# The first six A^T steps of the first pass are transposed and cast in the last block of the set-up, and written from SyncE's queue

## The chip, the cores and the metric

The kernel runs on one core of one Trainium2 chip. The time is the device time of one execution in microseconds (us). Engines are called as in the profile: PE is TensorE (PEld its weight loads), DVE is VectorE, ACT is ScalarE, POOL is GpSimd, SP is SyncE. SP only starts transfers here; POOL does small arithmetic and starts transfers too. All times inside an execution are counted from the start of the profiled span.

## The reference, cut to what matters

Two layers work on 4096 nodes with 512 features each. Layer 0 is a graph attention with 8 heads of 64 features over a 4096 x 4096 adjacency matrix of zeros and ones; layer 1 is an attention inside 32 groups of 128 nodes. The change touches layer 0 only:

```
feats   = einsum('nf,hfo->hno', X, W)                 # per head
s_self  = einsum('hno,ho->hn', feats, a_self)
s_neigh = einsum('hno,ho->hn', feats, a_neigh)
dense   = s_self[:, :, None] + s_neigh[:, None, :]
dense   = where(dense > 0, dense, 0.2 * dense) * A
attn    = softmax(dense, axis=-1)
out     = relu(concat_heads(attn @ feats) + b)
x       = layernorm(x + out)
```

Layer 1 then computes `layernorm(x + softmax(...) @ value)` with scores that are masked to the own group.

## The kernel before

**Layer 0 is streamed over the transposed adjacency matrix.** The exponentials of the two scores are taken once per node, so that a product of two exponentials stands for each entry, and a comparison ("mark") says on which side of the leaky ReLU an entry is. The kernel makes four passes, `main_pass(0)` to `main_pass(3)`, each for one pair of heads. A pass has four chunks `c` of 1024 target nodes, and a chunk has 32 steps `j` of 128 source nodes. One step needs `ats[r, c, j]`, a 128 x 1024 float32 tile of A^T.

**How a tile of A^T comes about.** In the first pass `bring(0, c, j)` makes two steps at once: eight PE transposes (L1122) of an fp8 block `a_b`, with two fp8 values taken as one bf16 value, into one PSUM bank that `misc` hands out; then two ACT copies (L1126, "CAST at<-ps_m") that widen them to float32 in SBUF; then, for each, a write to the scratch tensor `at_d` in HBM (L1127, started by POOL). In later passes `bring` only reads `at_d` back through SP. The block `a_b` is loaded by POOL in `load_adjacency` (L596); the first three are requested in blocks 3, 4 and 5 of the set-up.

**What a step does with it.** DVE computes `q` (L1361), two of them per step; ACT (L1370) or, for one in eight, DVE (L1366) computes the marks; PE then runs matmuls into `accf` (L1381, 4 per step, needs only the A^T tile), `acc` (L1401, 16 per step, needs `q`), `dens` (L1415, needs the marks) and, in the first pass, `ae` (L1325). In the first three passes the steps are taken in groups of eight (`wide=8`): all `accf` matmuls of a group, half of the next group's `bring`, all `acc` matmuls, the `dens` and `ae` matmuls, the other half of `bring`. Only the first group of all has no group ahead of it that could bring its tiles. It does so itself, before its first matmul:

```
                if at_step == 0:
                    for j in cycle:
                        bring(0, 0, j)
```

**The set-up ahead of the first pass** has eight blocks `k` of four row tiles. In each block PE computes features of tile `u` (`features(k, u)`, 4 matmuls, L743), DVE adds the bias (`fb`, L751), DVE and ACT make two scaled copies (`gst`, L757; `fst`, L765 and L766), and POOL writes them to HBM (`g_d`, `f_d`, L778). `exponentials`, `scores`, `turn_rows`, `rows_of_exponentials` and `columns_of_exponentials` stand between them. After the last block (k = 7) PE has `sums_to_columns` (L583) and `columns_of_exponentials(7)` (L735); DVE reads these from PSUM (`S_col` L819, `pu_all` L736), clears `dens` (L826), and the PSUM banks of the set-up go over to the passes.

**What sets the order.** PE runs its instructions exactly in program order (`manual_schedule`). For ACT, DVE, POOL and SP a planner fixes the order when the program is built, from program order and from when it reckons an operand to be ready, and it moves later work ahead where it sees a gap: the loads `p_row<-pu_d` and `f_s<-f_d` of the first pass are started from 42 us on, in the middle of the set-up.

**Buffers.** The `at` tiles have six buffers (`atp`) that exist from the beginning, and six more (`at2`) that are allocated when the set-up's SBUF pools are closed; `ring` takes them in turn, so steps 0 to 5 use the first six, steps 6 and 7 the later ones. `q` has six early and two later buffers. During the set-up `misc` has one PSUM bank, from the first pass on two. `fst`, `gst` and `fb` have three buffers each in the set-up, so the fourth tile waits until the first has been written to HBM.

Of the kernel before, what the change touches and what calls it, by code (L numbers as in the profile page):

```python
# [10 lines left out]
F32 = mybir.dt.float32  # L11
BF16 = mybir.dt.bfloat16
# [7 lines left out]
P = 128  # L20
# [375 lines left out]
F32R = mybir.dt.float32r  # L396
# [8 lines left out]
def adjacency_streamed_path(  # L405
# [29 lines left out]
    nc = tc.nc  # L435
# [8 lines left out]
    FP8 = mybir.dt.float8e4  # L444
    C = 1024
    CT = C // P
# [18 lines left out]
    at_d = dram.tile([NCH, NT, P, C], F32, name="at_d")  # L465
# [30 lines left out]
    ident_b = const.tile([P, P], BF16, name="ident_b")  # L496
# [49 lines left out]
    atp = ctx.enter_context(tc.tile_pool(name="at", bufs=6))  # L546
# [10 lines left out]
    def misc(shape, dtype=F32):  # L557

        banks.append(banks.pop(0))
        return banks[-1].tile(shape, dtype, name="ps_m")  # L560

    turns = {"at": 0, "q": 0}
    more = {}

    def ring(name, pool, n):

        if name not in more:
            return pool
        k = turns[name] % (n + more[name][1])
        turns[name] += 1  # L570
        return pool if k < n else more[name][0]

    def partial_sums(dst, wide, rhs):

        for c in range(FC):
            nc.tensor.matmul(
                dst[32 * c : 32 * c + 32, :], wide[:, c, :32], rhs[:, c, :], start=True, stop=True
            )
# [8 lines left out]
    ats = {}  # L587
    a_bs = {}
# [3 lines left out]
    def load_adjacency(c, j):  # L592

        a_b = pools["adj"].tile([P, CT, 4 * P], FP8, name="a_b8")
        a_bs[c, j] = a_b
        return nc.gpsimd.dma_start(  # L596
            a_b, adj[ts(c, C), j * P : (j + 4) * P].rearrange("(t p) n -> p t n", p=P)
        )


    with tc.tile_pool(name="setup1", bufs=1, side="right") as one, tc.tile_pool(
        name="setup2", bufs=2, side="right"
    ) as two, tc.tile_pool(name="setup3", bufs=3, side="right") as three, tc.tile_pool(
        name="xtp", bufs=4, side="right"
    ) as xtp, tc.tile_pool(name="ps_setup", bufs=7, space=PSUM) as pss:
        NB = NT // 4
        xts, xTs, sts, pu_js, rows = {}, {}, {}, {}, {}

        def tile_j(x, u):

            return x.rearrange("p (q n k) -> p q n k", q=2, k=2)[:, u // 2, :, u % 2]

        def load_rows(k):
            xts[k] = []
            for u in range(4):
                xt = xtp.tile([P, F], F32, name="xt_f")
                nc.sync.dma_start(xt, x[ts(4 * k + u, P), :])
                xts[k].append(xt)
# [34 lines left out]
        def turn_rows(k):  # L653
            xT = xTs[k] = two.tile([P, FC, 4, P], F32, name="xT_f")
            pts = {}

            order = [(u, c) for u in range(4) for c in range(FC)]
            for u, c in order if k == 0 else sorted(order, key=lambda x: x[1]):
                if u == 0:
                    pts[c] = pss.tile([P, 4, P], F32, name="ps_set")  # L660
                nc.tensor.transpose(pts[c][:, u, :], xts[k][u][:, ts(c, P)], ident)
            for c in range(FC):
                pt = pts[c]
                nc.scalar.activation(
                    xT[:, c], pt, AF.Identity, accum_out=xs[:, c, k : k + 1]
                )

        def scores(k):

            ps = pss.tile([P, 4 * P], F32, name="ps_set")  # L670
            for c in range(FC):
                nc.tensor.matmul(
                    ps[32 * c : 32 * c + 32, :],
                    wa[:, c, :],
                    xTs[k][:, c].rearrange("p u n -> p (u n)"),
                    start=True,
                    stop=True,
                )
            st = sts[k] = one.tile([P, 4 * P], F32, name="st")
            nc.scalar.copy(st, ps)  # L680
# [38 lines left out]
        def rows_of_exponentials(k):  # L719
            pr = pss.tile([2 * H, 4, P], F32, name="ps_set")  # L720
            for u in range(4):
                nc.tensor.transpose(
                    pr[:, u, :], pu_js[k][:, u].rearrange("p k h -> p (k h)"), ident
                )
            row = rows[k] = one.tile([2 * H, 4 * P], F32, name="pu_row")
            nc.scalar.copy(
                row.rearrange("p (q n k) -> p q k n", q=2, k=2),
                pr.rearrange("p (q k) n -> p q k n", q=2),
            )
            nc.gpsimd.dma_start(pu_d[:, ts(k, 4 * P)], row)  # L730

        def columns_of_exponentials(k):
            pc = pss.tile([P, 4, 2 * H], F32, name="ps_set")
            for u in range(4):
                nc.tensor.transpose(pc[:, u, :], rows[k][:, ts(u, P)], ident[: 2 * H, : 2 * H])  # L735
            nc.vector.tensor_copy(  # L736
                pu_all[:, 4 * k : 4 * k + 4].rearrange("p u k h -> p u (k h)"), pc
            )

        def features(k, u):  # L740
            pf = pss.tile([P, H * FH], F32, name="ps_set")
            for c in range(FC):
                nc.tensor.matmul(  # L743
                    pf,
                    tile_j(xTs[k][:, c].rearrange("p u n -> p (u n)"), u),
                    w_sb[:, c, :],
                    start=(c == 0),
                    stop=(c == FC - 1),
                )
            fb = three.tile([P, H, FH], F32, name="fb")  # L750
            nc.vector.tensor_add(fb.rearrange("p h o -> p (h o)"), pf, b_row)  # L751
            return fb

        def scaled_features(k, u, fb):
# [19 lines left out]
            for dst, n, src in (  # L774
# [2 lines left out]
            ):  # L777
                nc.gpsimd.dma_start(dst[:, k, :, ts(u, n)].rearrange("r p n -> p r n"), src)  # L778

        turn_rows(0)  # L780
        for k in range(NB):
            if k + 1 < NB:
                load_rows(k + 1)
            fbs = [features(k, 0)]
            if k == 0:
                fbs.append(features(k, 1))
                scores(0)
            else:
                exponentials(k)
            if k + 1 < NB:  # L790
                turn_rows(k + 1)
            if k == 0:
                exponentials(0)
            scaled_features(k, 0, fbs[0])
            if k:
                fbs.append(features(k, 1))
                columns_of_exponentials(k - 1)
            scaled_features(k, 1, fbs[1])
            fbs.append(features(k, 2))
            scaled_features(k, 2, fbs[2])  # L800
            if k + 1 < NB:
                scores(k + 1)
            rows_of_exponentials(k)
            if k == NB - 1:
                xsum = one.tile([P, FC], F32, name="xsum")
                nc.vector.tensor_reduce(xsum, xs, AX.X, OP.add)
                xsum_b = one.tile([P, FC, 32], F32, name="xsum_b")
                nc.vector.tensor_copy(xsum_b, xsum[:, :, None].to_broadcast([P, FC, 32]))
                pS = pss.tile([P, H * FH], F32, name="ps_set")
                partial_sums(pS, xsum_b, w_sb)  # L810
                S_part = one.tile([P, H * FH], F32, name="st")
                nc.scalar.copy(S_part, pS)
            fbs.append(features(k, 3))
            scaled_features(k, 3, fbs[3])
            if k in (3, 4, 5):
                tc.keep_in_program_order(load_adjacency(0, 4 * (k - 3)))
# [288 lines left out]

    checked = []

    def bring(r, c, j):

        if r:  # L1110
            at = ats[r, c, j] = ring("at", atp, 6).tile([P, C], F32R, name="at")
            nc.sync.dma_start(at.bitcast(F32), at_d[c, j])
            return
        if j % 2:
            return
        if j % 4 == 0 and (c, j) not in a_bs:
            load_adjacency(c, j)
        pairs = a_bs[c, j - j % 4].rearrange("p t n -> p (t n)").bitcast(BF16)
        pairs = pairs.rearrange("p (t k n) -> p t k n", t=CT, k=2)[:, :, j % 4 // 2, :]
        pt = misc([P, CT, P], BF16)  # L1120
        for t in range(CT):
            nc.tensor.transpose(pt[:, t, :], pairs[:, t, :], ident_b)  # L1122
        both = pt.rearrange("p t n -> p (t n)").bitcast(FP8).rearrange("p (n k) -> p n k", k=2)
        for k in range(2):
            at = ats[r, c, j + k] = ring("at", atp, 6).tile([P, C], F32R, name="at")
            nc.scalar.copy(at, both[:, :, k])  # L1126
            nc.gpsimd.dma_start(at_d[c, j + k], at.bitcast(F32))  # L1127

    def load_block():

        k = len(checked)
# [168 lines left out]
    def main_pass(r, ae=None, wide=4):  # L1300

        for c in range(NCH):
# [33 lines left out]
            for j0 in range(0, NT, wide):  # L1336
# [9 lines left out]
                    nc.sync.dma_start(g_s[k].rearrange("p u h o -> p (u h o)"), g_d[r, k])  # L1346
                if at_step == 0:
                    for j in cycle:
                        bring(0, 0, j)
                follow = [  # L1350
                    x
                    for x in steps[at_step + wide : at_step + 2 * wide]
# [110 lines left out]
    with tc.tile_pool(name="lp", bufs=2) as lp, tc.tile_pool(  # L1463
        name="lp1", bufs=1
# [58 lines left out]
```

## Time and profile before

| | before |
|---|---|
| median of 3 timed runs (lowest, highest) | 2079.16 us (2077.47, 2079.18) |
| the profiled execution, span from its first to its last instruction | 2080.8 us |
| PE busy in the span | 2045.7 us, 98% |
| DVE busy | 1660.4 us, 80% |
| ACT busy | 1536.7 us, 74% |
| POOL busy | 246.4 us, 12% |
| mean granted PE clock | 0.996 |
| set-up, up to the last PE instruction of it | about 163 us |
| first pass | about 163 to 600 us |

The profiled execution is one execution of its own, and its span is the only time given for it; it is 1.6 us above the median of the timed runs. Busy time of an engine is the union of its instructions. A line of the waits reads: the engine and what it wrote, what it waited for, the total in us, how often, and the longest. A line of the chain reads: start in us, length in us, what ran, and how many instructions of it.

### The profile page before, as it was taken

Reading aid. Unit: us, or ns where it says so; the run is one execution under the profiler, and the core shown is the slowest. Engines: PE = TensorE matmul, PEld = TensorE weight load, DVE = VectorE, ACT = ScalarE, POOL = GpSimd, SP = SyncE. Lnnn points to the kernel's source line nnn. Section 1 sums busy time; section 2 is a strip of 40 time slices with the busy share of each in tenths; the row PEclk is TensorE's granted clock in tenths of the full one; section 3 lists DMA queues with packets and bytes.
Section 4 is the critical chain, followed back from the end, with each engine's and each line's share of the span. In section 5 each row is a group of like instructions: output and inputs, shape, how many; then the busy total and the mean of one; then the engine's idle time right before and its main releaser. Section 6 shows DMA issues by size and latency. Waiting matters only on the chain.

```text
span 2080.8 us, 38068 instructions
## 1 busy us (share of the span) xinstructions
PE 2045.7 (98%) x14982; PEld 1005.3 (48%) x14982; DVE 1660.4 (80%) x2040; ACT 1536.7 (74%) x1821; POOL 246.4 (12%) x393
## 2 busy tenths in 40 slices
PE   8999999999999999999999999999999999999997
PEld 4555555454445544444445444444454444445443
DVE  5557887878799998798999999999975984886654
ACT  3338888888878989788899889998885666567420
POOL 2343222222100000000000000000200210210111
PEclk9999999999999999999999999999999999999999
DMA  8999999999899999888999999989974764775211
GB/s 249 267 257 247 270 292 259 296 260 285 261 326 342 347 346 337 275 303 285 323 317 334 310 344 331 330 288 363 321 242 138 247 250 129 227 272 167 72 48 43
DMA packets 207881, 551.28 MB, mean 265 GB/s; under 512 B 25292, under 2 KB 66252, under 8 KB 207692
## 3 DMA queue, kind: packets, MB, share of 16 engines
q1 hardware_dynamic: 140748, 425.79, 59.0%
q0 software_dynamic: 62784, 121.91, 23.3%
q8 instruction: 120, 1.97, 0.4%
q10 hardware_dynamic: 4160, 1.05, 0.2%
q14 instruction: 69, 0.57, 0.1%
HBM read 491.79 MB, written 107.22 MB: 288 GB/s over the span
## 4 chain that ended last, share of the span: by engine, by line
PE 83%; DMA 7%; issue 4%; DVE 2%; ACT 2%; POOL 1%; SPq 0%; POOLq 0%; ACTq 0%; DVEq 0%
PE acc L1401 36%; PE accf L1381 20%; PE ps_set L743 5%; PE ps_m L1059 5%; DMA at_d<-at 5%; PE ps_m L987 5%; PE dens L1415 5%; PE ps_m L1014 1%; PE ps_m L1073 1%; ACT mark L1370 1%; DVE q L1361 1%; PE ps_m L1122 1%; PE ps_m L916 1%; DMA f_s<-f_d 1%; DMA hs_d<-hst 1%
## 5 line engine op out<-in xcount | busy, mean ns | idle before, releaser
L1361 DVE SCALAR_TENSOR_TENSOR q<-p_row,d_all,at 128x1024 f32<-128x1024 f32 x1024 | 1242.0, 1278 | 171.4 <-PE acc L1401 143.7
L1370 ACT ACTIVATE mark<-q,nb_all 128x1024 fp8e4<-128x1024 f32 x896 | 994.6, 1145 | 176.1 <-DVE q L1361 160.3
L1401 PE MATMUL acc<-q,g_s 128*32 128x512 f32 x8192 | 903.0, 593 | 1.1 <-DVE q L1361 0.4
L1401 PEld LDWEIGHTS acc<-q,g_s 128*32 128x32 f32 x8192 | 264.5, 110 | 594.1 <-issue 533.1
L1381 PE MATMUL accf<-at,f_s 128*128 128x512 f32 x2048 | 494.5, 397 | 2.3 <-issue 1.8
L1381 PEld LDWEIGHTS accf<-at,f_s 128*128 128x128 f32 x2048 | 379.9, 189 | 111.7 <-issue 29.1
L1141 ACT ACTIVATE ck<-ck,neg_half_f 128x1024 f32<-128x1024 f32 x128 | 146.0, 1140 | 20.5 <-DMA ck<-in_adj_dram 20.5
L1142 ACT ACTIVATE ck<-ck,neg_quarter 128x1024 f32<-128x1024 f32 x128 | 146.3, 1143 | 1.8
L1126 ACT CAST at<-ps_m 128x1024 fp32r<-128x1024 fp8e4 x128 | 120.2, 1025 | 12.3 <-issue 5.9
L1415 PE MATMUL dens<-mark,e_b 128*6 128x512 fp8e4 x2048 | 125.4, 379 | 2.7 <-ACT mark L1370 2.7
L743 PE MATMUL ps_set<-w_sb_f,xT_f 128*128 128x512 f32 x256 | 116.9, 605 | 0.1
L987 PE MATMUL ps_m<-x1T,M_sb 128*128 128x512 f32 x256 | 113.1, 595 | 1.6 <-ACT x1T L968 1.6
L1059 PE MATMUL ps_m<-wvT,x1T 128*128 128x512 f32 x256 | 114.2, 594 | 0.0
L1246 POOL DMA_DIRECT2D hs_d<-hst x12 | 10.7, 895 | 832.9 <-DVE hst L1236 739.0
L1366 DVE TENSOR_SCALAR mark<-q,d_all 128x1024 fp8e4<-128x1024 f32 x128 | 95.7, 748 | 4.8
L1415 PEld LDWEIGHTS <-e_b 128*6 128x6 bf16 x2048 | 52.7, 86 | 83.0 <-issue 38.8
L1127 POOL DMA_DIRECT2D at_d<-at x128 | 68.8, 538 | 178.0 <-ACT at L1126 111.0
L765 ACT ACTIVATE fst<-fb 128x512 fp32r<-128x512 f32 x32 | 20.3, 636 | 85.3 <-DVE fb L751 48.3
L987 PEld LDWEIGHTS ps_m<-x1T,M_sb 128*128 128x128 f32 x256 | 47.9, 190 | 63.1 <-issue 60.1
L1059 PEld LDWEIGHTS ps_m<-wvT,x1T 128*128 128x128 f32 x256 | 47.6, 190 | 57.2 <-issue 56.0
L743 PEld LDWEIGHTS ps_set<-w_sb_f,xT_f 128*128 128x128 f32 x256 | 49.0, 199 | 51.3 <-issue 49.9
L994 ACT ACTIVATE zT<-ps_m,zb 128x512 f32<-128x512 f32 x32 | 21.8, 683 | 70.3 <-PE ps_m L987 70.3
(185 smaller groups left out, 1119.2 us busy)
## 6 DMA issues: line engine op xcount, KB each, us to landing
at<-at_d SPq DMA_DIRECT2D x384, 512.0 KB, 6.0
ck<-in_adj_dram SPq DMA_DIRECT2D x128, 512.0 KB, 5.5
f_s<-f_d SPq DMA_DIRECT2D x128, 512.0 KB, 7.4
at_d<-at POOLq DMA_DIRECT2D x128, 512.0 KB, 14.8
g_s<-g_d SPq DMA_DIRECT2D x128, 256.0 KB, 5.6
f_d<-fst POOLq DMA_DIRECT2D x32, 512.0 KB, 7.7
p_row<-pu_d SPq DMA_DIRECT2D x32, 512.0 KB, 6.7
a_b<-in_adj_dram POOLq DMA_DIRECT2D x32, 512.0 KB, 16.8
```

Source lines behind the costliest of these rows:

```text
L743: nc.tensor.matmul(pf, tile_j(xTs[k][:, c].rearrange("p u n -> p (u n)"), u), w_sb[:, c, :], start=(c == 0), stop=(c == FC - 1),)
L987: nc.tensor.matmul(pz, L1["M"][:, f, ts(c, P)], x1T[:, f, :], start=(f == 0), stop=(f == FC - 1),)
L1059: nc.tensor.matmul(pv, x1T[:, f, ts(u, P)], L1["wvT"][:, f, :], start=(f == 0), stop=(f == FC - 1),)
L1126: nc.scalar.copy(at, both[:, :, k])
L1141: tc.keep_in_program_order(nc.scalar.activation(ck, ck, AF.Square, bias=neg_half))
L1142: nc.scalar.activation(ck, ck, AF.Abs, bias=neg_quarter, accum_out=binp[:, k : k + 1])
L1361: nc.vector.scalar_tensor_tensor(q, p_row[h], d_j, ats[r, c, j].bitcast(F32), op0=OP.max, op1=OP.mult)
L1366: nc.vector.tensor_scalar(mark, q, d_j, None, op0=OP.is_gt, saturate=False)
L1370: nc.scalar.activation(mark, q, AF.Sigmoid, bias=nb_all[:, j, hh : hh + 1], scale=BIG, saturate=False,)
L1381: nc.tensor.matmul(accf[:, s, :], f_s[j // 4][:, j % 4, w, :], ats[r, c, j][:, ts(s, HB)], start=(j == 0 and w == 0), stop=(j == NT - 1 an ...
L1401: nc.tensor.matmul(acc[o : o + 32, s, :], g_s[j // 4][:, j % 4, h, o % FH : o % FH + 32], qs[j, h][:, ts(s, HB)], start=(j == 0), stop=(j ...
L1415: nc.tensor.matmul(dens[lo : lo + 6, :], e_b[:, j, 2 * r + h, :], marks[j, h][:, ts(s, HB)], start=(j == 0), stop=(j == NT - 1),)
```

## The change

`bring` is moved, unchanged but for one argument, ahead of the set-up; the argument names the queue that starts the write of A^T (POOL as before, unless told otherwise). In the last block of the set-up (k = 7) a new function calls it three times, for steps 0 and 1 after the features of tile 0, for steps 2 and 3 after the features of tile 1, for steps 4 and 5 ahead of the features of tile 3, each with SP as the queue of the two writes. The counter of the ring of `at` buffers is moved on by two each time, since the six later buffers don't exist yet. The first group of the pass then brings only what is missing, steps 6 and 7.

```diff
+    def bring(r, c, j, queue=nc.gpsimd):
+
+        if r:
+            at = ats[r, c, j] = ring("at", atp, 6).tile([P, C], F32R, name="at")
+            nc.sync.dma_start(at.bitcast(F32), at_d[c, j])
+            return
+        if j % 2:
+            return
+        if j % 4 == 0 and (c, j) not in a_bs:
+            load_adjacency(c, j)
+        pairs = a_bs[c, j - j % 4].rearrange("p t n -> p (t n)").bitcast(BF16)
+        pairs = pairs.rearrange("p (t k n) -> p t k n", t=CT, k=2)[:, :, j % 4 // 2, :]
+        pt = misc([P, CT, P], BF16)
+        for t in range(CT):
+            nc.tensor.transpose(pt[:, t, :], pairs[:, t, :], ident_b)
+        both = pt.rearrange("p t n -> p (t n)").bitcast(FP8).rearrange("p (n k) -> p n k", k=2)
+        for k in range(2):
+            at = ats[r, c, j + k] = ring("at", atp, 6).tile([P, C], F32R, name="at")
+            nc.scalar.copy(at, both[:, :, k])
+            queue.dma_start(at_d[c, j + k], at.bitcast(F32))
...
+        def early_steps(k, j):
+
+            if k == NB - 1:
+                bring(0, 0, j, nc.sync)
+                turns["at"] += 2
+
         turn_rows(0)
         for k in range(NB):
             if k + 1 < NB:
                 load_rows(k + 1)
             fbs = [features(k, 0)]
+            early_steps(k, 0)
             if k == 0:
                 fbs.append(features(k, 1))
                 scores(0)
@@
             scaled_features(k, 0, fbs[0])
             if k:
                 fbs.append(features(k, 1))
+                early_steps(k, 2)
                 columns_of_exponentials(k - 1)
             scaled_features(k, 1, fbs[1])
             fbs.append(features(k, 2))
@@
                 nc.scalar.copy(S_part, pS)
+            early_steps(k, 4)
             fbs.append(features(k, 3))
             scaled_features(k, 3, fbs[3])
...
-    def bring(r, c, j):
...
-            nc.gpsimd.dma_start(at_d[c, j + k], at.bitcast(F32))
...
                 if at_step == 0:
                     for j in cycle:
-                        bring(0, 0, j)
+                        if (0, 0, j) not in ats:
+                            bring(0, 0, j)
```

More of the change, by code (lines that the diff above doesn't have):

```diff
@@ L1106, in adjacency_streamed_path @@
     checked = []
-    def bring(r, c, j):
[L1110 to L1126, printed above, removed]
-            nc.gpsimd.dma_start(at_d[c, j + k], at.bitcast(F32))
     def load_block():
```

## The prediction, made before the changed kernel was run

> **What bounds the kernel now.** I first read the busy times of the page, then the waits of PE over the whole span:
>
> ```profile
> span 2080.8 us, 38068 instructions
> PE 2045.7 (98%) x14982; PEld 1005.3 (48%) x14982; DVE 1660.4 (80%) x2040; ACT 1536.7 (74%) x1821; POOL 246.4 (12%) x393
> ...
> PE ps_m L1122 <- ACT at L1126: 3.0, 2, 1.8
> PE dens L1415 <- ACT mark L1370: 2.7, 5, 0.7
> ...
> PE acc L1401 <- DVE q L1361: 0.4, 2, 0.2
> PE accf L1381 <- DMA f_s<-f_d: 0.4, 1, 0.4
> ```
>
> PE is busy 98% of the span and its waits are few, so time taken off PE's path should show at the end. One of the largest waits belongs to the change: PE waits 3.0 us, in two pieces, for the casts of A^T. The chain of waits around the seam between set-up and first pass shows where:
>
> ```profile
> 161.83 0.80 PE ps_set L583 x8
> ...
> 163.43 0.14 DVE pu_all L736
> 163.57 0.04 issue
> 163.62 0.62 PE ps_m L1122 x8
> ...
> 164.46 0.63 ACT fst L765
> 165.09 2.74 ACT at L1126 x3
> 167.83 0.04 issue
> 167.87 1.01 PE ps_m L1122 x8
> 168.88 9.61 PE accf L1381 x32
> 178.49 0.91 PE ps_m L1122 x16
> 179.40 14.07 PE acc L1401 x127
> ```
>
> For a few us ACT leads the path, with casts and one set-up copy. Then 32 accf matmuls take 9.61 us. In the first pass's undisturbed groups the same chain gives 7.39 us for 32. The table by stretches says why (us; PE, PEld, DVE, ACT, POOL busy; granted PE clock; DMA share; GB/s):
>
> ```profile
> 149.00:163.00 14.00, 14.00 (x57) 6.84 (x57) 9.32 (x25) 3.44 (x10) 5.81 (x8) 1.00 0.78 252
> 163.00:169.00 6.00, 2.86 (x33) 2.49 (x33) 4.82 (x8) 5.45 (x7) 3.67 (x6) 0.81 0.61 211
> 169.00:179.00 10.00, 10.00 (x44) 7.88 (x44) 6.89 (x6) 9.97 (x10) 3.93 (x6) 0.77 1.01 352
> ```
>
> Cut by single microseconds, the clock goes from 1.00 to 0.50 inside 166 to 167 us and back inside 173 to 174: 6.8 us at half speed, following the idle PE. In the set-up's last block, 149 to 163 us, PE is full but ACT is busy for only 3.44 of 14 us, then it is full until 180.
>
> **What the Trainium skill says.** "TensorE: Matmul & The Clock Gate", Part 1 (the HAM clock gate), puts the window after which an idle PE falls to half clock at about 3.4 us, and the same for recovery. The trace agrees: the slow stretch is 6.8 us, two windows. "ScalarE: Activation LUTs", section on what ACT_TABLE_LOAD costs, gives 1283 ns per load; here one load of 1.28 us stands at 169.67 us, ahead of the first mark. "DMA: Bandwidth & Descriptors", section "Issuing engines are not separate DMA queues", says transfers share the same 16 engines whoever starts them, so SP saves POOL issue time and no transfer. The trace before has no at_d write from SP to compare.
>
> **The change part by part.** I follow PE from the end of the set-up's own work (L735 starts at 162.55, lasts 0.41: 162.9 us) to the end of the first accf matmuls, 178.49: 15.6 us.
>
> *What this stretch would take undisturbed:* four sets of eight transposes at 0.50 us (16 take 1.00 in steady groups), 2.0 us, and accf 7.4: 9.4. So 6.2 us are lost: 1.8 + 1.2 idle for casts, 2.2 by half clock in accf, 0.5 by it in the last transposes, the rest (about 0.4) at the hand-over of PSUM.
>
> *Moved transposes.* Three sets go into the block: 3 x 0.50 = 1.5 us there and 1.5 less behind it, sum 0. With the chain's 0.62 per set the block would pay 1.9; cost between 0 and 0.4, I take 0.
>
> *Moved casts.* Six at 0.95 to 1.02 us, some 6 us, into ACT's 10.6 idle us of the block. The bank must be free for the next set: between the first and second sets PE has exponentials 0.84 and features 3.54, 4.4 us, against two casts of 2.0, copies of 0.6 and exponentials of 0.5; between second and third 5.4 us (0.35 + 3.64 + 0.44 + 1.00). So PE waits for none, cost 0. Behind a cast on ACT wait the exponentials (L695 to L700), up to 2 us later: what needs them, the transposes L722 of pu_j, comes 7 us later. S_part (L812) is needed by L583 3 us after its copy; two casts ahead of it use 2 of these. Without this cover each late us of a cast costs PE one.
>
> *Moved writes.* Six POOL issues of 0.54 us (3.2 us) leave POOL. SP has no transfer to start between 115.6 and 170.97 us, so its waits for casts hold back nothing. The bytes are another matter: 6 x 0.52 = 3.1 MB come before 163 us. At 252 GB/s for a share of 0.78 the full rate is some 323, so 14 us have room for about 1.0 MB, and 163 to 169 for 0.8 (0.39 x 6 x 346). The rest queues. The f_d writes then land late; they took 4.6 to 4.9 us in the quiet and up to 11.1 under load. The fst copy of tile 2 (158.10) needs the f_d issued at 149.78, so at 9.7 us (the median from 130 to 150) it waits 1.4 us on ACT; PE's next need of ACT is at 163.2 (L583), so that is hidden, but with 11.1 us and two casts behind it, PE could lose about 1.
>
> *What is late next.* PE would have steps 0 to 5 at hand at 162.9 + 1.5 = 164.4, transposes steps 6 and 7 until 164.9, and waits for the PSUM banks: pu_all (ends 163.57, now 1.5 later) releases at 165.1, cost 0.2. Without the pause there is no half clock. Then the casts of steps 6 and 7: their buffers lie where set-up pools were. SP's bv_row load, also into freed space, waited for the last f_d until 170.97. If these two casts wait for that f_d as well (now about 170.6, because its fst no longer stands behind a cast), they end at 171.6 and 172.6, step 7's four matmuls (0.9) end at 173.5, not 172.5: cost 1.0. If not, 0. If the planner fills early q and marks ahead of fst, 1.3 more. I take 0.9.
>
> *Sum:* 6.2 - 0.2 - 0.9 = 5.1 us gained, the span 2080.8 - 5.1 = 2075.7. The timed median stands 1.6 under the profiled span, so I subtract from the median: 2079.16 - 5.1 = **2074.0 us**. The neighbouring engines allow it: ACT has six casts fewer (5.7 us) from 163 us on, so its marks come as much earlier as PE asks. DVE needs 16 q at 1.2 and two marks at 0.75, 20.7 us, per group of 25.8. If q only starts at 166.3 as now, the last is ready at 187, acc ends at about 189.1 instead of 193.47: 4.4 gained. But six q buffers exist early, casts come from 150 us on and DVE idles for 4.7 of 14 us, so I expect some q in the block. Step 12's block `a_b` is released earlier, which hurts nobody.
>
> **The rivals.**
>
> *A, half the gain.* The q start late, or the last two casts wait for a late f_d (landing at 172.5: accf ends at 175.3, 3.2 gained), or the PSUM bank costs PE 1 us in the block. For it: DMA share 1.01 from 169 on. Against: DVE and ACT idle in the block. Gain 3.2 to 4.1: 2075.0 to 2076.0.
>
> *B, given back.* From 302 to 502 us the chain runs six times through at_d landings of 11 to 16 us each, to hs_d<-hst (11.75) and an ACT copy; PE then waits 1.6 us at 405 and 1.1 at 515, for marks. If that chain and not PE paces the pass, an earlier start waits there: 2079.2. Against: PE waits only 2.7 us in 430, and 3.1 MB of the transfers are now done ahead of the pass, which is why these waits may as well shrink (up to 2.7 more gained, 2071.3).
>
> *C, slower.* The same place with the other sign: the planner, given other starting times, sets hs_d or a copy on POOL or ACT further behind at the three inner chunk ends, each delay stopping PE at dens. From 1.7 us more per end (5.1 / 3) the gain is gone; 4 us more, a third of an hs_d landing, gives 2079.2 + 12 - 5.1 = 2086. For it: ACT has only 2 us to spare in a group (busy 23.45 of 25.8), so delays aren't recovered at once. Against: the first chunk end, at 297 us, has no such wait.
>
> *That it doesn't do what it says:* the three calls are in PE's program order, so the transposes do move; only casts could be planned late, which is case A.
>
> **How the numbers follow.** Forecast (gain over 4.2) 0.56, A 0.20, B given back 0.08, C 0.16. 0.2% of the time is 4.2 us, about what a measurement of this kernel can tell from no change. So faster 0.56, same 0.28, slower 0.16. The range from 2071.3 (waits of the pass gone as well) to 2079.5 holds forecast, A and B and leaves out C and little else. The likeliest case's own range is 2071.3 to 2075.0.
>
> **What would show it right or wrong.** In the changed profile: 24 transposes before 162 us with no PE wait for a cast; no clock of 0.5 between 160 and 200 us; the chain's accf at about 7.4 us, ending at 172.5 to 173.5; casts of steps 0 to 5 before 163 us; six at_d writes from SP; the first acc ending near 188; the waits for marks not above 2.7 us. Wrong would be PE idle in the block, a wait of accf for the casts of steps 6 and 7 over 1 us, or waits of dens for marks that grow by several us.

## The result, and the profile after

The change made the kernel slower.

| | before | after |
|---|---|---|
| median (lowest, highest), 6 runs each | 2079.35 us (2077.47, 2080.57) | 2092.51 us (2089.56, 2097.38) |
| ratio, 95% interval | | 1.0061 [1.0052, 1.0071] |
| the profiled execution, its span | 2080.8 us | 2092.4 us |
| mean granted PE clock | 0.996 | 0.993 |

13.2 us were lost by the medians, 11.6 by the spans; 5.1 us of gain had been forecast. In what follows the lines of the new kernel have its own numbers: the casts "at" are L619, `accf` is L1391, `q` L1371, `fst` L787, `f_d` L799, `pu_d` L751, the load of `a_b` L596.

The page's first lines and the waits of PE over the span, of the kernel after:

```profile
span 2092.4 us, 38056 instructions
PE 2046.1 (98%) x14982; PEld 1004.1 (48%) x14982; DVE 1659.6 (79%) x2040; ACT 1537.3 (73%) x1821; POOL 244.1 (12%) x387
```

```profile
PE accf L1391 <- ACT at L619: 15.9, 1, 15.9
...
PE dens L1425 <- ACT mark L1380: 2.0, 3, 0.7
...
PE ps_m L997 <- DVE tot L914: 1.5, 1, 1.5
```

The two waits for casts (3.0 us in all) are gone, and one of 15.9 us, in one piece, has come: `accf` waits for a cast. The waits for marks and the one for `tot` have not grown (2.7 and 2.3 us before), so the loss is this one place. The chain of waits of the kernel after, around the seam (start, length, what):

```profile
178.39 7.00 DMA f_d<-fst
...
185.65 1.02 ACT at L619
...
186.71 3.78 PE accf L1391 x8
190.49 1.73 PE ps_m L615 x16
192.22 13.89 PE acc L1411 x128
206.12 1.73 PE dens L1425 x32
```

The first `accf` matmuls end at 190.49, against 178.49 before: 12.0 us later, about the whole of the loss. The table by stretches, of the kernel after, has the columns of the prediction's table (PE, PEld, DVE, ACT, POOL busy; granted PE clock; DMA share; GB/s):

```profile
149.00:163.00 14.00, 14.00 (x64) 6.98 (x63) 13.08 (x26) 13.37 (x21) 6.18 (x8) 1.00 0.99 278
163.00:169.00 6.00, 5.73 (x38) 4.83 (x37) 1.97 (x5) 3.22 (x4) 1.65 (x2) 1.00 1.13 258
169.00:179.00 10.00, 1.77 (x8) 1.13 (x6) 2.63 (x4) 1.15 (x1) 0.61 (x1) 0.81 1.10 236
179.00:190.00 11.00, 3.29 (x8) 2.48 (x8) 2.10 (x3) 1.93 (x2) 1.25 (x3) 0.50 0.66 177
```

The block does what was forecast: PE is full from 149 to 163 us, and from 163 to 169 it loses 0.27 us at full clock where it had 2.86 of 6 us busy before. Then it stands still. The DMA columns are the new thing: the engines are full from 149 us on (0.99 to 1.13, where they had been at 0.78 and 0.61), and yet each full share moves *less*: 278 GB/s at 0.99, then 258 at 1.13 and 236 at 1.10, where the kernel before moved 352 at 1.01. (A share above 1 is read here as packets of one engine that overlap.)

Why the last `f_d` is so late is read from two lists in order of time. First POOL's transfers, kernel before:

```profile
158.49 0.53 POOL L730 DMA_DIRECT2D pu_d<-pu_row  x1 [2.15 <-ACT pu_row L726]
...
166.11 0.75 POOL L778 DMA_DIRECT2D f_d<-fst  x1 [0.70 <-DVE fst L766]
...
174.74 1.81 POOL L596 DMA_DIRECT2D a_b<-in_adj_dram  x2
```

and after (start, length; in brackets the idle time before it and what ended that):

```profile
153.89 1.11 POOL L596 DMA_DIRECT2D a_b<-in_adj_dram  x1
...
159.16 0.53 POOL L751 DMA_DIRECT2D pu_d<-pu_row  x1
...
165.05 0.90 POOL L596 DMA_DIRECT2D a_b<-in_adj_dram  x1 [2.70 <-PE ps_m L615]
165.94 0.76 POOL L799 DMA_DIRECT2D g_d<-gst  x1
178.39 0.75 POOL L799 DMA_DIRECT2D f_d<-fst  x1 [11.69 <-DVE fst L787]
```

Two loads of `a_b`, those of steps 12 and 16, have moved. A block of `a_b` serves four steps; as its transposes now run in the set-up, the first buffer is free 11 us earlier (153.6 us, 164.2 before) and the second 4 us (164.7, 168.9 before), and the planner starts each next load at once, 21 and 10 us earlier than before, ahead of `pu_d` and of the last `f_d`. Then DVE's list, kernel after:

```profile
164.75 0.22 DVE L757 COPY pu_all<-ps_set 128x64 f32<-128x64 f32 x1
176.21 1.28 DVE L1371 SCALAR_TENSOR_TENSOR q<-p_row,d_all,at 128x1024 f32<-128x1024 f32 x1 [11.24 <-DMA pu_d<-pu_row]
177.41 0.68 DVE L787 SCALAR_TENSOR_TENSOR fst<-fb,fst 128x512 fp32r<-128x512 f32 x1
```

The seventh `q`, the first in a later buffer, stands ahead of the set-up's last `fst` and waits 11.24 us for the landing of `pu_d`, a write of 32 KB started at 159.16. By the answer on that tile it took 16.9 us to land, against 2.2 before. So there are two suspects on the way to `f_d`, the loads and DVE's order, and behind it the casts of steps 6 and 7, whose buffers, by the order of the pools in the kernel, lie where `fst` was.

### The profile page after: what moved, and what is told of

It is laid out like the page before. It is cut to its first block, busy times and chain, and to the rows that moved or that the text cites. A ratio compares the mean times of both kernels' runs of the same rounds, so it can differ in the third digit from the quotient of the medians.

```text
span 2092.4 us, 38056 instructions
## 1 busy us (share of the span) xinstructions
PE 2046.1 (98%) x14982; PEld 1004.1 (48%) x14982; DVE 1659.6 (79%) x2040; ACT 1537.3 (73%) x1821; POOL 244.1 (12%) x387
## 3 DMA queue, kind: packets, MB, share of 16 engines
HBM read 491.79 MB, written 107.22 MB: 286 GB/s over the span
## 4 chain that ended last, share of the span: by engine, by line
PE 80%; DMA 5%; issue 2%; DVE 2%; ACT 2%; POOL 0%; POOLq 0%; SPq 0%; ACTq 0%; DVEq 0%
PE acc L1411 38%; PE accf L1391 21%; PE ps_m L1089 5%; PE dens L1425 5%; PE ps_m L1017 5%; DMA at_d<-at 3%; PE ps_m L1044 1%; PE ps_m L1103 1%; DVE q L1371 1%; PE ps_m L615 1%; ACT mark L1380 1%; PE ps_m L946 1%; DMA hs_d<-hst 1%; PE ps_m L997 1%; PE ps_m L1244 1%
## 5 line engine op out<-in xcount | busy, mean ns | idle before, releaser
L1371 DVE SCALAR_TENSOR_TENSOR q<-p_row,d_all,at 128x1024 f32<-128x1024 f32 x1024 | 1243.0, 1280 | 189.8 <-PE acc L1411 149.1
L1391 PE MATMUL accf<-at,f_s 128*128 128x512 f32 x2048 | 493.9, 397 | 18.0 <-ACT at L619 15.9
L1391 PEld LDWEIGHTS accf<-at,f_s 128*128 128x128 f32 x2048 | 379.5, 188 | 126.9 <-issue 25.3
L619 ACT CAST at<-ps_m 128x1024 fp32r<-128x1024 fp8e4 x128 | 120.1, 1023 | 21.3 <-DMA f_d<-fst 6.9
```

The costliest lines, as they stand in the source:

```text
L1371: nc.vector.scalar_tensor_tensor(q, p_row[h], d_j, ats[r, c, j].bitcast(F32), op0=OP.max, op1=OP.mult)
L1391: nc.tensor.matmul(accf[:, s, :], f_s[j // 4][:, j % 4, w, :], ats[r, c, j][:, ts(s, HB)], start=(j == 0 and w == 0), stop=(j == NT - 1 an ...
```

## The experiments

Three theories, by the letters of the expectations. **H**: the order on DVE; the seventh `q` stands in front of `fst`, and with `q` behind `fst` or an early `pu_d` the time comes back. **B**: the `a_b` loads; they stand ahead of `pu_d` and `f_d` in POOL's queue and take the DMA engines, and with them behind the last `f_d` the time comes back. **S**: the six early writes from SP crowd the DMA engines. Each run is compared with runs of the kernel before on the same chip, whose medians were 2081.6, 2082.7, 2081.1 and 2079.8 us in the four series; only ratios are compared across series. The diffs show the deciding lines; those that remember the last `fst` and `f_d` (`last`), and the helper that hands out `at` buffers from two pools, are left out.

### The seventh q behind fst

```diff
+    held = at_step == 0 and j >= 3
+    with tc.issue_after(last["fst"].ins) if held else nullcontext():
         nc.vector.scalar_tensor_tensor(q, p_row[h], d_j, ats[r, c, j]...)
```

> The changed kernel, with the q of steps 3 to 7 of the first group kept behind the set-up's last fst on VectorE; the order of ScalarE, GpSimd and SyncE stays as it is. Theory H (VectorE's queue: the seventh q stands ahead of the last fst and waits 11.2 us for the landing of pu_d): fst runs at about 165.5 us instead of 177.4, its f_d is started near 167 instead of 178.4, lands near 173, and TensorE's wait for the casts of steps 6 and 7 falls from 15.9 us to 4 or less; span about 2080. Theory B (GpSimd's transfer queue: two a_b loads are started earlier and the last f_d stands behind the second of them, which landed at 183.4 us): f_d is started early but lands no earlier than about 184, so the wait stays above 13 us; span 2089 to 2093. Theory S (SyncE's A^T writes crowd the transfers): as B, landing late.

2093.58 us, ratio 1.0061 [1.0046, 1.0076], as slow as the kernel after. The chain of waits of this run:

```profile
155.26 17.62 DMA a_b<-in_adj_dram
...
173.40 14.13 DMA f_d<-fst
...
187.78 1.02 ACT at L620
```

and the start of `f_d` in POOL's list:

```profile
173.40 0.75 POOL L800 DMA_DIRECT2D f_d<-fst  x1 [5.33 <-DMA a_b<-in_adj_dram]
```

DVE did `fst` early (167.6), and it helped nothing: POOL could not start `f_d` for 5.3 us because an `a_b` load, eight transfers earlier in its queue, had not landed, and then `f_d` took 14.13 us. It landed at 187.5 (185.39 in the kernel after), and PE waited 16.7 us. H falls: DVE's order only decides which of two waits is seen.

### pu_d started from SP

```diff
-            nc.gpsimd.dma_start(pu_d[:, ts(k, 4 * P)], row)
+            queue = nc.sync if k == NB - 1 else nc.gpsimd
+            queue.dma_start(pu_d[:, ts(k, 4 * P)], row)
```

> The changed kernel, with the pu_d write of the last block started from SyncE instead of GpSimd. H: pu_d lands within 5 us, about 164, the seventh q no longer holds VectorE, the last fst runs by 167, TensorE's wait is 4 us or less; span about 2080. B: VectorE is free, but f_d still stands behind the second a_b load and lands near 184; the wait stays above 13 us; span 2089 to 2093. S: as B.

2096.27 us, ratio 1.0074 [1.006, 1.0089]. The chain of waits:

```profile
158.82 8.15 DMA pu_d<-pu_row
...
169.28 18.23 DMA f_d<-fst
```

From SP, `pu_d` lands in 8.15 us and no longer in 16.9; so more than half of its delay was its place behind POOL's loads. The `q` then ran at 167.1 and `f_d` started at 169.28, nine us earlier than in the kernel after. It landed at 187.5 all the same, behind the second `a_b`. H falls a second time.

### The a_b loads behind the last f_d

```diff
+        held = c == 0 and j >= 12
+        with tc.issue_after(last["f_d"].ins) if held else nullcontext():
             return nc.gpsimd.dma_start(a_b, adj[...])
```

> The changed kernel, with the a_b loads of steps 12 and 16 kept behind the set-up's last f_d in GpSimd's queue (in the kernel before they were started at 174.7 us, in the changed one at 153.9 and 165.1); nothing else moves on VectorE, ScalarE and SyncE. B: pu_d lands within 8 us of its start, by 167, the seventh q waits 2 us or less, f_d is started by 169 and lands by 175, TensorE's wait for the casts falls from 15.9 to 0 to 4 us; time 2073 to 2079, the gain that was forecast or most of it. H alone: VectorE's order is the same, so the wait stays near 16 us unless pu_d lands early; 2090. S: SyncE's writes are all still there, so pu_d and f_d still land 15 us or more after their start; 2088 or more.

2082.87 us, ratio 1.0003 [0.9995, 1.0012]: of the 0.61% lost, 0.58 are back with nothing but POOL's order changed, while the six writes still start from SP. B holds, and S falls as the cause of the loss. But B's own figures were missed in part: `f_d` landed at 177.74 and not by 175, the wait is 6.8 us and not 4 at most, and the gain is still missing. The wait of PE over the span, that of ACT between 160 and 200 us, and the chain:

```profile
PE accf L1396 <- ACT at L622: 6.8, 1, 6.8
```

```profile
ACT at L622 <- DMA f_d<-fst: 8.1, 1, 8.1
```

```profile
169.60 8.14 DMA f_d<-fst
...
178.04 1.02 ACT at L622
...
179.11 3.73 PE accf L1396 x8
```

The casts of steps 6 and 7 still wait for `f_d`, now landing at 177.74; PE waits 6.8 us for them, and pays half clock on top (0.50 granted from 178 to 182 us): 3.73 us for eight matmuls that take a quarter of 7.4 in a steady group.

### The early writes from POOL

```diff
-                bring(0, 0, j, nc.sync)
+                bring(0, 0, j)
```

> The changed kernel with its six early A^T writes started from GpSimd, as before the change, instead of SyncE. The planner then puts both a_b loads behind the last f_d by itself, and the last fst ahead of the seventh q. B: TensorE's wait is 0 to 5 us, since only six plain writes stand ahead of f_d in the queue; time 2073 to 2080. S: also fast, and faster than the variant that only delays the a_b loads by 2 us or more. If the move of casts and transposes itself were the cost, this run would stay above 2088.

2085.25 us, ratio 1.0016 [1.0009, 1.0023]; the expected 2073 to 2080 was missed. It isn't a test of the queue alone: given the longer queue on POOL, the planner itself put both `a_b` loads behind `f_d` and `fst` ahead of the seventh `q`. That it then loses a wait of the same kind (7.0 us for the casts) fits B, and it says that SP as the queue did no harm.

### Later pools in the other order

`more_q` is allocated ahead of `more_at`, so that the `at` buffers move up by two.

```diff
-    at2 = ...tile_pool(name="more_at", bufs=MORE)
     q2 = ...tile_pool(name="more_q", bufs=2)
+    at2 = ...tile_pool(name="more_at", bufs=MORE)
```

> The changed kernel, with the two later SBUF pools allocated in the other order: the two later q buffers come to lie over the set-up's fst, and the six later A^T buffers further on. The a_b loads stay early. Theory B in its second half (steps 6 and 7 are cast into SBUF that the last fst still holds until its f_d has landed): the casts of steps 6 and 7 no longer wait for f_d, they run by 168 us, TensorE's first 32 accf matmuls end near 173 without a wait over 1 us. But the seventh q now waits for f_d, which stands behind the early a_b loads and lands near 184, and the acc matmuls of step 3 wait for it until about 186: TensorE loses about 7 us there; span 2080 to 2086, better than the changed kernel and no better than before. If the casts had another reason to wait, accf still waits 15 us and the span stays at 2091.

> The changed kernel with both: the a_b loads of steps 12 and 16 behind the last f_d, and the two later pools in the other order. Theory B: f_d lands at 175 to 178 us, only the seventh q waits for it, and acc needs that q at about 178; TensorE waits 1 us or less for casts and 2 us or less for q; the clock stays at full speed between 160 and 200 us; the gain is what the prediction's sum had, 4 to 6 us: 2074 to 2077 where the kernel before takes 2079 to 2081, a ratio of 0.997 to 0.998. If the moved casts, transposes or writes themselves cost something that these waits have hidden, the ratio stays at 1.000 or above.

> The kernel before the change, with the two later pools in the other order; the order of instructions on every engine is that of the kernel before. Every theory: within 0.1% of the kernel before, 2079 to 2081, since there the casts of steps 6 and 7 came at 172 us, after f_d had landed at 170.95. If it is faster by 3 us or more, the order of the pools helps by itself and the run with both edits says less about the change.

`swap` (one run, the loads still early) took 2095.24 us with a wait of 16.6 us for the casts: the expectation missed. Two `q` are 8 KB per partition, less than the 24 KB of `fst`, `fb` and `gst`; so, by the sizes in the kernel, the `at` pool still began on the room of these, and the casts still waited for `f_d`. `ab_swap`, with the loads late, took 2082.81 us, 1.0003 [0.9993, 1.0012]: no better than `ab_late` where 0.997 to 0.998 had been expected, with a wait of 3.7 us and the same half clock (3.78 us for the last eight `accf`). The control `before_swap` measured 0.9996 [0.999, 1.0003]: the order of the pools alone is worth nothing.

These waits suggest how buffers pass on. The seventh `q` of the kernel after waited for `pu_d`; in `swap` both the casts and that `q` waited for `f_d` (the `q` for 19.3 us). That fits one reading: a later pool waits here for every reader of an earlier pool that it touches, also where its own buffer does not lie over what is read. Which buffer lies over which is worked out from the kernel; no trace shows it, and the reading was not tested by itself. The next runs build on it.

### f_d started from SP

On top of `ab_late`, the last `f_d` is started by SP.

```diff
+                if j == NT - 1 and dst is f_d:
+                    nc.sync.dma_start(rows_out, src)
...
```

> The changed kernel with the a_b loads of steps 12 and 16 late, and the last f_d started from SyncE instead of GpSimd, so that it doesn't stand behind other transfers in GpSimd's queue. The wait that was left with late a_b loads alone was 6.8 us (f_d 8.1 us from start to landing). If that landing is long by the queue: it takes 5 us or less, the wait of accf for the casts of steps 6 and 7 is 3.5 us or less, span 2076 to 2079. If it is long because all transfers share the rate: still 7 to 8 us, wait 5 us or more, span about 2082.

2086.54 us, 1.0021 [1.0013, 1.0028], slower than `ab_late`. `f_d` started at 167.48 and landed 10.2 us later, in spite of SP's queue; PE waited 7.5 us. The run changes two things: the loads are now held only behind the `f_d` before the last, so they start at 166.38, ahead of it. (The profile puts the casts' wait down to one of these loads, but that one landed 14.3 us after its start, later than the casts.) The Trainium skill, "DMA: Bandwidth & Descriptors", section "Issuing engines are not separate DMA queues", says that all transfers share the same 16 engines, whichever engine starts them, and this run agrees. The section adds that another engine saves only the time to start a transfer. For the 32 KB of `pu_d` that isn't what was measured: from SP it landed in 8.15 us and not in 16.9.

### The later pools clear of fst

The `at` buffers of steps 6 to 10 are laid beyond all of `fst`, `fb` and `gst`; the two later `q` and the last `at` buffer lie over them.

```diff
-    at2 = ...tile_pool(name="more_at", bufs=MORE)
     q2 = ...tile_pool(name="more_q", bufs=2)
+    at3 = ...tile_pool(name="more_at3", bufs=1)
+    at2 = ...tile_pool(name="more_at", bufs=MORE - 1)
```

> Two edits on the kernel after: the loads of `a_b` for steps 12 and 16 stand behind the set-up's last f_d in POOL's queue, and the later pools are laid so that the A^T buffers of steps 6 to 10 lie beyond the buffers of fst, fb and gst (five of the six in one pool from 180512 up, the sixth and the two q buffers below it). With a_b late alone, the casts of steps 6 and 7 waited 6.8 us for the landing of f_d. If that hand-over of memory is the last wait of the seam, these casts run as soon as pu_d has landed, by 169 us, the accf matmuls wait under 1 us for them, no stretch of half clock follows, accf ends by 174 us against 178.5 before, and the kernel takes 2075 to 2078, ratio 0.997 to 0.999: the forecast gain with both waits out of the way. If instead the gain is lost behind the seam, by q that wait for f_d in their turn or by loads of the pass, accf ends by 174 and the time is still 2081 to 2083. If the casts wait for another thing than that memory, they still run at 174 or later and PE waits 3 us or more.

> Only the pools of the kernel after are laid anew, as in the run before; the loads of `a_b` stay ahead of pu_d and f_d. The casts of steps 6 and 7 then no longer wait for f_d (landing 185.4 in the kernel after) but for pu_d, which lay behind the a_b loads and landed at about 176. So accf should wait 7 to 9 us for them and the time be 2084 to 2087. If the memory of fst is not what they wait for, PE waits 15 us or more as in the kernel after: 2091 to 2095.

> The early A^T writes start from POOL (where the planner then puts the a_b loads of steps 12 and 16 behind f_d) and the pools are laid anew. at_from_pool alone took 2085.3, with a wait of 7.0 us for f_d. If that memory is the last wait, as in the first run: casts of steps 6 and 7 by 169, no wait of accf over 1 us, 2076 to 2080. If POOL's own starts of the A^T writes hold pu_d back, these casts come at 171 or later and the time is 2080 to 2083.

> The kernel before with its pools laid anew, and nothing else by hand (the planner places a few marks and loads of the later pass otherwise). A control for the other three: if laying the pools anew is worth something by itself, for the casts of steps 6 and 7 no longer wait for f_d here either, at most the half-clock loss at the seam shrinks, 2077 to 2080; if the gain of the first run comes from the moved steps, this one takes 2081 to 2083, ratio 0.999 to 1.001.

| run | median us | ratio | PE's wait for the casts of 6 and 7 |
|---|---|---|---|
| `ab_pools` (loads late) | 2080.77 | 0.9998 [0.9992, 1.0005] | none over 0.2 |
| `pool_pools` (writes from POOL) | 2079.90 | 0.9994 [0.9986, 1.0002] | none over 0.2 |
| `pools` (loads early) | 2094.41, one run | | 7.0 |
| `before_pools` (control) | 2083.45 | 1.0015 [1.0007, 1.0023] | |

The casts of steps 6 and 7 are shown to have waited for memory: with another place for their buffers the wait is gone. But the gain was not there. `ab_pools` fell under its "lost behind the seam, by q that wait"; `pool_pools` lies just inside its expected 2076 to 2080, but its ratio shows no gain. The control came out 0.15% slower than the kernel before, more than expected, so this layout may itself cost something. DVE's waits between 160 and 200 us in `pool_pools` (total, times, longest), and its list there:

```profile
DVE q L1378 <- DMA at_d<-at: 8.6, 1, 8.6
```

```profile
167.12 0.69 DVE L794 SCALAR_TENSOR_TENSOR fst<-fb,fst 128x512 fp32r<-128x512 f32 x1
176.38 2.48 DVE L1378 SCALAR_TENSOR_TENSOR q<-p_row,d_all,at 128x1024 f32<-128x1024 f32 x2 [8.57 <-DMA at_d<-at]
```

DVE stands for 8.57 us in front of the seventh `q`, whose buffer is now meant to lie over `fst`. (The profile names a write of `at_d` as what ended the wait; the last `f_d`, started at 168.10, landed 8.2 us later, at 176.3, the same moment. The next run decides between them.) `accf` ended at 173.51, as forecast, but the second group's `accf` began at 194.81, only 2.5 us before the kernel before's 197.27.

`pools` alone is the sharpest miss: PE's wait shrank to 7.0 us as expected, and the time stayed at 2094. There the same `q` waits until `f_d` lands at 190.8. DVE's list and POOL's show the wait, and why `f_d` was late once more:

```profile
191.04 2.48 DVE L1378 SCALAR_TENSOR_TENSOR q<-p_row,d_all,at 128x1024 f32<-128x1024 f32 x2 [22.37 <-DMA f_d<-fst]
```

```profile
179.87 0.55 POOL L627 DMA_DIRECT2D at_d<-at  x1 [11.62 <-ACT at L626]
180.41 0.75 POOL L806 DMA_DIRECT2D f_d<-fst  x1
```

The write of step 6, which needs the cast, which needs `pu_d` (17.3 us to land behind the early loads), stood ahead of `f_d` in POOL's queue. So, in this one run, the pools are of no use while the loads are in the way.

### The later q clear of fst as well

```diff
+    at3 = ...tile_pool(name="more_at3", bufs=3)
-    at2 = ...tile_pool(name="more_at", bufs=MORE)
+    at2 = ...tile_pool(name="more_at", bufs=3)
     q2 = ...tile_pool(name="more_q", bufs=2)
```

Steps 6 to 8 and both later `q` lie beyond `fst`; steps 9 to 11, not needed before the second group, lie over it.

> As pool_pools (early A^T writes from POOL), with the pools laid so that the A^T buffers of steps 6 to 8 and both later q buffers lie beyond fst, fb and gst, and the A^T buffers of steps 9 to 11 below. The seventh q then waits for pu_d (by 168 us) and no longer for f_d (176.4 in pool_pools). If that wait holds the rest of the gain: no idle time of DVE over 2 us after 168, the first group's acc ends by 188.5 us, the second group's accf starts by 193 (194.8 in pool_pools, 197.3 before), and the time is 2075 to 2078, ratio 0.9975 to 0.9985. If the pass gives it back further on, the second group starts by 193 and the time is still 2079 to 2081. If another thing than memory holds the q, they start at 175 or later again and the time is 2079 to 2081.

> As ab_pools (loads of a_b for steps 12 and 16 behind the last f_d, early A^T writes from SP), with the pools of the run before. If the wait of the seventh q for f_d holds the rest: second group's accf by 193, 2076 to 2079, ratio 0.9975 to 0.999. Otherwise 2080 to 2082 as ab_pools.

> The kernel before with the same pools and nothing moved, as control: 2080 to 2084, ratio 0.999 to 1.002, as before_pools (1.0015). If it is faster by over 0.1%, the pools and not the moved steps make the gain.

| run | median (lowest, highest) us | ratio |
|---|---|---|
| `pool_pools3` | 2074.64 (2074.00, 2077.89) | 0.9972 [0.996, 0.9984] |
| `ab_pools3` | 2076.98 (2074.06, 2079.70) | 0.9985 [0.9976, 0.9994] |
| `before_pools3` | 2081.64 (2078.68, 2082.66) | 1.0003 [0.9995, 1.0012] |
| before | 2079.81 (2077.87, 2083.64) | |

The wait of the seventh `q` for `f_d` is gone, and with it the rest of the loss: `pool_pools3` is faster than the kernel before, by 5.2 us of medians (2079.81 - 2074.64), and the pools alone are worth nothing. Its chain of waits at the seam:

```profile
164.93 0.14 DVE pu_all L764
...
165.12 7.60 PE accf L1398 x32
172.72 0.91 PE ps_m L622 x16
173.63 13.87 PE acc L1418 x128
187.50 1.73 PE dens L1432 x32
189.23 0.90 PE ae L1341 x16
190.13 1.00 PE ps_m L622 x16
191.13 7.41 PE accf L1398 x32
```

No wait from 165 us on, and the 32 `accf` in one piece at full clock (7.60 us, 7.41 in the next group). The second group's `accf` begins at 191.13, 6.1 us before the kernel before's. In the same stretch, DVE's waits no longer show memory; its `q` waits for PE to give a buffer back:

```profile
DVE q L1378 <- PE acc L1418: 3.7, 1, 3.7
```

Whether the 2.3 us between the two repaired kernels are real is not settled; their intervals overlap.

## Why the prediction was wrong, point by point

**The step that failed is "Step 12's block `a_b` is released earlier, which hurts nobody."** The moved transposes bring two more instructions forward, the loads into the buffers they free, and these were not followed to POOL's queue. Their size can be read from single microseconds of the kernel after, in the columns of the table above; the first two lie inside an `a_b` load, the last, taken later, inside two writes of `at_d` and the load of `bv_row` (256 KB, landing in 3.4 us):

```profile
163.00:164.00 1.00, 1.00 (x13) 0.98 (x11) 1.00 (x2) 1.00 (x2) 0.00 (x0) 1.00 1.17 163
164.00:165.00 1.00, 0.75 (x12) 0.55 (x10) 0.97 (x4) 1.00 (x2) 0.00 (x0) 1.00 1.23 102
188.00:189.00 1.00, 1.00 (x3) 0.72 (x3) 0.00 (x0) 0.00 (x0) 0.42 (x1) 0.50 1.00 391
```

While such a load runs, full DMA engines move 102 GB/s, against 391 later. An estimate from these: a load that lands 512 KB (524,288 bytes) takes 5.1 us of all sixteen engines (at 102), a write of 512 KB 1.3 us (at 391). The load turns float32 into fp8, so that 512 KB landed are 2 MB read, and the profile's page bears this out: it gives 491.79 MB read from HBM over the execution, and all transfers that read HBM make together 441.5 MB if the 32 `a_b` loads count as landed, 491.8 if each counts four times. So 102 GB/s landed are some 408 read, close to the 391. The six writes that the prediction counted are 3.1 MB, by the same rate 8 us of DMA, against free room of 5.4 us (0.22 x 14 + 0.39 x 6) between 149 and 169. Two loads add 10.3 us that it didn't count: instead of 2.6 us too many there were 12.9. That this is near the 12.0 us lost fits, but is only an estimate; what is shown is that moving these two loads alone brings 0.58% back, 12 us. The price could have been read before the change. The 9.7 us that the prediction took for an `f_d` is the median from 130 to 150 us, and the kernel before started its third `a_b` load in that stretch, at 133.60. From its transfers there (KB each, us to landing):

```profile
a_b<-in_adj_dram POOLq DMA_DIRECT2D x1, 512.0 KB, 11.7
pu_d<-pu_row POOLq DMA_DIRECT2D x1, 32.0 KB, 9.2
```

The same 32 KB landed in 2.2 us at 158.49, with no load under way.

**The term "the casts of steps 6 and 7", taken at 0.9 us, was mis-sized as well, and it is where the loss was paid.** The mechanism was named rightly, that they wait for the last `f_d`; but `f_d` was put at a landing of 170.6. It landed at 185.39, and with the loads out of the way still at 177.74 in `ab_late`, where the term measures 6.8 us of waiting and 1.9 of half clock (3.73 for eight `accf`, less a quarter of 7.4). That write started at 169.60 there, 3.5 us later than in the kernel before (166.11). Its `fst` no longer stood behind a cast, as the prediction said, but on ACT behind three early marks (164.02 to 167.15) and on DVE behind the seventh `q`; the prediction had left early `q` and marks ahead of `fst` as a chance, at 1.3 us.

**What was not in the sum at all:** the later `q` buffers. The prediction had "the last is ready at 187" for the `q` as a margin of DVE's, and did not ask on which earlier pool these two buffers lie. The difference between `pool_pools` and `pool_pools3` is 0.9994 - 0.9972 = 0.22%, some 4.6 us. Not all of it need be this wait: the two controls differ by 0.12% as well (1.0015 and 1.0003), and in the traces the time from the end of the first `accf` to the second group's is 21.3 us in `pool_pools` (173.51 to 194.81) and 18.4 in `pool_pools3` (172.72 to 191.13), 2.9 us less.

**Right:** the moved transposes and casts cost nothing in the block (PE 14.00 of 14.00 us); the early `q` filled DVE's gaps (13.08 of 14 us busy, 9.32 before); the writes from SP held back nothing and shared the rate; no half clock between 160 and 169; marks and `tot` wait no longer than before, so rivals B (given back from 302 us on) and C (delays at the inner chunk ends) are not what happened. Rival A named a late `f_d`, but let it land at 172.5 at most. No rival had a load that overtakes; the outcome lay outside the range.

**The sum itself holds once the three waits are out of the way.** Forecast: `accf` at 7.4 us ending at 172.5 to 173.5, first `acc` ending near 188, 5.1 us gained. `pool_pools3`: 7.60 us, ending at 172.72, `acc` ending at 187.50, 5.2 us gained. That the two gains agree to 0.1 us is chance: the interval of this run reaches from 3.3 to 8.3 us, and `ab_pools3`, the change with its writes on SP, gives 3.1 by its ratio. The prediction described the compute engines of the change rightly and its transfers and memory wrongly.

**Two readings that were off, without weight in the sum.** The chain from 302 to 502 us passes seven landings of `at_d`, not six. And the trace before does not agree with a window of 3.4 us as plainly as was said: no idle piece of PE ahead of the fall of the clock was longer than 1.82 us, and full clock came back some 5.7 us after PE took up work at 167.87. Read from single microseconds, the fall came some 4.4 us after PE's last matmul in the kernel after and 3.5 in `ab_late`, the return some 5.5 and 3.5 us after PE began again.

## What to carry to other kernels

A step that is moved earlier frees its operands earlier, and whatever refills them moves too: list the transfers that a release triggers, count their cost in DMA time (not in bytes landed), and look at what they now stand ahead of in their queue. Where buffers are taken over from closed pools, ask for each new buffer which old pool it touches and which transfer reads that pool last; work that is made earlier runs into these waits, which were hidden before. And when one wait is taken away and the time doesn't move, look at the next engine in the same stretch before giving up the gain: here three waits lay behind one another, and only with all of them gone did a gain of 3 to 5 us appear.

## What the runs showed of the hardware

- A load that converts float32 to fp8 held the DMA engines at a share of 1.23 with 102 GB/s moved; with two writes of `at_d` and a plain load under way they reached 391. By the HBM bytes on the profile's page the converting load reads four times what it lands. A write of 32 KB behind such loads in POOL's queue took 16.9 us to land (2.2 before the change), 8.15 when SP started it. The Trainium skill, "DMA: Bandwidth & Descriptors", section "SWDGE vs HWDGE vs iDMA", says that transfers which cast can only be started by GpSimd and that one queue is allocated to it; the profile's page of this kernel shows one such queue too, so these loads always share it with POOL's small writes.
- POOL waited 5.3 us (5.2 in `swap`) at the start of a transfer until the one eight places earlier in its queue had landed. That eight is the limit is read from these two places only.
- After 15.9 us without work PE ran at a granted clock of 0.50, and eight `accf` took 3.78 us, twice a quarter of the 7.41 of a steady group.
